# Keys of later chunks carried in the first low-rank step as well, and the activations transferred twice

## The chip, the cores and the metric

One NeuronCore of a Trainium2 chip runs the whole kernel. Its engines work side by side: TensorE (PE, with its weight loads shown apart as PEld), VectorE (DVE), ScalarE (ACT), GpSimd (POOL) and SyncE (SP), which issues nearly all DMAs. The metric is the device time of one execution in microseconds, as the median of several runs.

## The reference, cut to what matters

The block is a transformer layer on x of shape (2, 2048, 256), float32 throughout: a modulated layer norm, causal linear attention with 16 heads of width 16 and 128 random features, a residual, a second modulated norm, and a feed-forward layer of 1024 hidden channels with four low-rank experts of which two are taken.

```python
phi_q, phi_k = phi(q), phi(k)          # exp(x @ omega - |x|^2/2) / sqrt(128)
S = cumsum(phi_k[..., :, None] * v[..., None, :], axis=2)
Z = cumsum(phi_k, axis=2)
y = einsum('bhtm,bhtmd->bhtd', phi_q, S) / (einsum('bhtm,bhtm->bht', phi_q, Z)[..., None] + 1e-6)
x = x + ga * (y @ W_proj + b_proj)
h = layernorm(x) * (1 + cb) + sb
base, lora = h @ Wi.T, (h @ A) @ B     # lora for each of four experts
out = sum over the two best experts of  w_e * (relu(base + lora_e) @ Wo.T)
x = x + gb * out
```

## The kernel before, in words

The 4096 tokens are cut into N = 8 blocks of 512 tokens (four chunks of 128). Heads are taken in NG = 4 groups of four. A block has 16 (group, chunk) steps, done two chunks at a time: PAIRS = 8 pairs, one for each value of k in the main loop over i (block) and k (pair); the text calls one turn of that loop a slot. In slot (i, k) the attention of pair k of block i is finished, the scores of the following pair are prepared, and beside it run pieces of the neighbours: projections of block a = i + 1, norm, router and the first hidden unit of p = i - 1, the remaining hidden units of q = i - 2. Which piece stands where is written out by hand in run_full, and keep_written_order makes each engine run its instructions exactly as written. Every wait is therefore paid where it stands, with everything behind it on that engine.

A pair needs its keys turned, tokens by features. There are two ways. `turn` takes the exponentials phi and transposes them on TensorE (keys, L500), after which ScalarE copies them (keep_keys, L542). `key_rows` (L522) instead multiplies the raw key features once more by omega, with the operands the other way round, in the upper half of the four PSUM banks that a hidden unit uses, and ScalarE takes the exponential (keep_key_rows, L532). Key rows use 32 rows of the array for each head, as low_step (L821) uses 16, so the four heads run beside each other. In before only the second low-rank step of a unit carries them, for the pair that follows, in blocks 2 to 6 at k = 0, 1, 2 and 7 (these are the late slots).

From the turned keys, increments (L576) makes the change of the state into the upper half of the py bank, keep_increments (L588) copies it to SBUF (tile ds), states (L597) transposes it in the next slot and adds it to S (L607). outputs (L621, L627) makes the pair's result, keep_outputs (L635) copies it. Then features (L476) fills four mm banks for the next group and exponentials (L487) reads them.

A hidden unit is hidden (L836, 16 matmul instructions into four mm banks), first (low_step, then ReLU on ScalarE, L850) and second (low_step again, then max and scale on VectorE, L864, into one of four r buffers, and an addition on GpSimd, L865). Something is put between first and second so that TensorE has work while ScalarE reads the banks. PSUM tiles come from two rings: mm with four banks, side with two. A tile takes the ring's oldest bank, and its first writer waits until all readers of the bank's previous tile are done.

A block's x is loaded once, two blocks ahead (load, L99), into one of five xt buffers. It is used for the first norm (norm1), gets the projection's bias on GpSimd (add_bias, L370) at k = 6 of the block before, and is the residual in project (L682, L686) and finish (L874, L879) until store. At the end of the program, after the loop, come divide_invert of the last block (L660 to L666), three hidden units of block 6, divide (L675), project, norm2 and the rest of block 7.

Of the kernel before, what the change touches and what calls it, by code (L numbers as in the profile page):

```python
# [14 lines left out]
P = 128  # L15
# [17 lines left out]
def kernel(  # L33
# [58 lines left out]

    def load(i, pieces=1):
        b, blk = divmod(i, NBLK)
        xt = work.tile([P, NT, C], FP, tag="xt", name=f"xt{i}", bufs=5)
        src = x[b, blk * TB : (blk + 1) * TB, :].rearrange("(t p) c -> p t c", p=P)
        n = NT // pieces
        for t in range(0, NT, n):
            nc.sync.dma_start(xt[:, t : t + n, :], src[:, t : t + n, :])  # L99
        st[i] = {"x": xt}  # L100


    w_sb = const.tile([P, KC, 3 * C], FP, name="w_sb")
# [63 lines left out]

    def second_columns():

        second_row = work.tile([P, P], FP, tag="kt", name="second_row", bufs=1)  # L170
# [294 lines left out]
        )  # L465


    S, phi, turned, staged, y = {}, {}, {}, {}, {}

    def features(i, g, side):  # L470
        f = st[i]["feat"][side, g]
# [18 lines left out]
    def carried(i, t):  # L490

        return (i % NBLK, t) != (NBLK - 1, NT - 1)

    def keys(i, g, t, tile):

        if not carried(i, t):
            return
        pk = tile(f"pk{i}_{g}{t}")
        for j in range(HG):
            nc.tensor.transpose(  # L500
                pk[:, j * P : (j + 1) * P], phi[i, g, 1, j][:, t * P : (t + 1) * P], ident
            )
        turned[i, g, t] = pk
# [3 lines left out]
    def key_tile(i, g, t):  # L507

        n = (i, g, t // 2)
        if n not in pair:  # L510
            pair.clear()
            pair[n] = work.tile([P, 2, HG, M], FP, tag="kt", name=f"kt{i}_{g}{t}", bufs=1)
        return pair[n][:, t % 2]

    def key_rows(chunks, banks):


        for j, bank in enumerate(banks):
            rs = slice(2 * DH * j, 2 * DH * (j + 1))
            for i, g, t in chunks:  # L520
                c0 = TH + (t % 2) * P
                nc.tensor.matmul(  # L522
                    bank[:, c0 : c0 + P], st[i]["feat"][1, g][rs, t * P : (t + 1) * P], om[rs, :],
                    start=False, stop=True, skip_group_check=True, tile_position=(2 * DH * j, 0),
                )

    def keep_key_rows(chunks, banks):
# [36 lines left out]
        )  # L564
        staged[i, g, t] = am

    raised, before = {}, {}

    def increments(chunks, bank):

        cols = bank[:, TB // 2 : TB].rearrange("p (c m) -> p c m", m=P)
# [8 lines left out]
                )  # L580
        return ready, cols

    def keep_increments(ready, cols):
        if not ready:
            return
        i, g, t = ready[0]
        d = work.tile([P, 2, P], FP, tag="ds", name=f"ds{i}_{g}{t}")
        nc.vector.tensor_copy(d[:, 0 : len(ready), :], cols[:, 0 : len(ready), :])  # L588
        for n, chunk in enumerate(ready):
            raised[chunk] = d[:, n, :]  # L590
# [248 lines left out]
                )  # L839
        s["unit"][u] = (banks, f0, ts, whole_banks)  # L840

    def first(i, u):
        s = st[i]
        banks, f0, ts = s["unit"][u][0:3]
        low_step(s, 0, banks, f0, ts)
        for j, ph in enumerate(banks):
            f = f0 + j
            if f not in s["g"]:
                s["g"][f] = work.tile([P, TB], FP, tag="g", name=f"g{i}_{f}", bufs=NF)
            nc.scalar.activation(s["g"][f][:, ts], ph, AF.Relu)  # L850

    def second(i, u, chunks=()):

        s = st[i]
        banks, f0, ts, whole_banks = s["unit"].pop(u)
        if chunks:
            key_rows(chunks, whole_banks)
        low_step(s, 1, banks, f0, ts)
        if chunks:
            keep_key_rows(chunks, whole_banks)  # L860
        for j, ph in enumerate(banks):
            g = s["g"][f0 + j][:, ts]
            r = work.tile([P, TH], FP, tag="r", name=f"r{i}_{u}{j}", bufs=RG)
            nc.vector.scalar_tensor_tensor(r, ph, 0.0, s["rho"][:, ts], ALU.max, ALU.mult)  # L864
            nc.gpsimd.tensor_add(g, g, r)  # L865
# [77 lines left out]

    PAIRS = NG * NT // 2

    def run_full(i, k, turn, state, following):


# [20 lines left out]

        def unit_keys(of, which, *between):  # L970

            first(of, which)
# [97 lines left out]
    def behind(i, k):  # L1070
# [1 line left out]
        if 1 <= p < N and k == 5:  # L1072
            choose(p)
        if i + 2 < N:
            if k == 1 and i != 1:
                load(i + 2)
        if i == 0 and k == 6:
            load(3)
        if a < N and k == 6:
            if i == 0:  # L1080
                add_bias(0)
            add_bias(a)
        if i < N and k == PAIRS - 1:
            divide_load(i)

# [5 lines left out]
    for i in range(N):  # L1091
        for k in range(PAIRS):
# [146 lines left out]
```

## Time and profile before

| what | value |
|---|---|
| median of 3 runs | 758.28 us (758.04 to 760.54) |
| the profiled execution's own time | 756.79 us |
| its span, first to last instruction | 755.0 us |
| mean granted TensorE clock | 1.000 |
| instructions in the span | 24542 |
| key transposes L500 | 328, 137 ns of busy time each (44.9 us) |
| key rows L522 | 304, 47 ns each (14.4 us) |
| HBM | 35.32 MB read, 28.57 MB written |

A row of the timeline gives the start and the length in microseconds, the engine, the line of the kernel, the operation, the tiles written and read with their shapes, the number of instructions merged into the row, and in square brackets how long the engine stood idle before it and what released it. A row of the waits gives the engine and line that waited, what for, the total, the count and the longest. A matrix product in float32 is two instructions in the trace, a transpose one. Matmuls overlap in the array, so the length of one is not what it adds to a sequence: this text measures sequences from the start of one row to the start of another, most often on PEld.

### The profile page before, as it was taken

The numbers are of one execution on the slowest core, as the hardware profiler recorded it, in microseconds if no ns is written. First come the engines' busy times: TensorE is split into PE (matmuls) and PEld (weight loads), VectorE is DVE, ScalarE is ACT, GpSimd is POOL, SyncE is SP. The second block draws the span as 40 slices with busy tenths as digits, with TensorE's granted clock in tenths as the row PEclk, the third lists the DMA queues.
The fourth block names the chain that finished last, engine by engine and source line by source line (L and its number), as shares of the span: only waits on it lengthen the run. The fifth ranks groups of instructions, "written<-read, shape, count | busy, mean of one in ns | idle before, by whom it ended". The sixth has DMA issues, their size and how long they took to land.

```text
span 755.0 us, 24542 instructions
## 1 busy us (share of the span) xinstructions
PE 744.8 (99%) x10720; PEld 552.1 (73%) x10720; DVE 407.0 (54%) x1133; ACT 329.6 (44%) x742; POOL 148.3 (20%) x192
## 2 busy tenths in 40 slices
PE   9999999999999999999999999999999999999998
PEld 6667776666787767776787677877688777777776
DVE  5667667564663547534656456645364424654612
ACT  1665546535544444435544455435454343521010
POOL 3000322222210322011220122103130112005122
PEclk9999999999999999999999999999999999999999
DMA  4369443123301433023420342204240130002000
GB/s 134 111 195 298 146 143 100 44 82 120 114 29 32 129 112 114 17 72 119 124 72 33 111 125 82 67 29 130 73 127 16 50 110 17 16 34 83 1 29 28
DMA packets 44234, 65.46 MB, mean 87 GB/s; under 512 B 6752, under 2 KB 20256, under 8 KB 44128
## 3 DMA queue, kind: packets, MB, share of 16 engines
q1 hardware_dynamic: 42240, 62.33, 26.1%
q8 instruction: 84, 1.38, 0.8%
q10 hardware_dynamic: 1888, 1.58, 0.7%
q14 instruction: 22, 0.18, 0.1%
HBM read 35.32 MB, written 28.57 MB: 85 GB/s over the span
## 4 chain that ended last, share of the span: by engine, by line
PE 93%; DVE 4%; ACT 1%; issue 1%; DMA 0%; POOL 0%; DVEq 0%
PE ph L836 13%; PE pf L874 12%; PE pa L552 9%; PE pp L476 9%; PE pq L384 7%; PE ph L821 4%; PE pk L500 4%; PE pv L457 4%; PE py L621 4%; PE py L576 4%; PE py L627 3%; PE po L682 3%; PE pt L597 3%; PE pf L896 2%; PE ph L522 2%; PE pta L331 1%
## 5 line engine op out<-in xcount | busy, mean ns | idle before, releaser
L865 POOL TENSOR_TENSOR g<-g,r 128x256 f32<-128x256 f32 x128 | 90.6, 741 | 416.3 <-DVE r L864 416.3
L487 ACT ACTIVATE phi<-pp,lnm 128x512 f32<-128x512 f32 x256 | 155.2, 689 | 9.7 <-PE pp L476 3.6
L874 PE MATMUL pf<-wo_g,g 128*128 128x256 f32 x448 | 103.6, 382 | 0.4 <-ACT phi L487 0.2
L836 PE MATMUL ph<-h,wi_sb 128*128 128x256 f32 x448 | 101.9, 380 | 0.1
L836 PEld LDWEIGHTS ph<-h,wi_sb 128*128 128x128 f32 x448 | 84.3, 190 | 12.5 <-DVE r L864 0.5
L874 PEld LDWEIGHTS pf<-wo_g,g 128*128 128x128 f32 x448 | 82.6, 190 | 13.7 <-issue 2.2
L552 PEld LDWEIGHTS pa<-phi,phi 128*32 128x32 f32 x4096 | 77.5, 110 | 14.8 <-issue 13.3
L552 PE MATMUL pa<-phi,phi 128*32 128x128 f32 (+3 forms) x4096 | 85.4, 235 | 0.1
L850 ACT ACTIVATE g<-ph 128x256 f32<-128x256 f32 x112 | 33.9, 389 | 115.1 <-PE ph L821 115.1
L635 ACT COPY y<-py 128x128 f32<-128x128 f32 x128 | 27.8, 269 | 125.2 <-DVE ds L588 123.4
L561 DVE TENSOR_TENSOR am<-pa,causal 128x512 f32<-128x512 f32 x128 | 81.8, 681 | 0.0
L391 DVE TENSOR_SCALAR qs<-pq,bqk 128x512 f32<-128x512 f32 x30 | 22.5, 751 | 99.3 <-PE pq L384 94.6
L476 PE MATMUL pp<-f,om 32*128 32x512 f32 x512 | 73.6, 640 | 0.0
L542 ACT COPY kt<-pk 128x512 f32<-128x512 f32 x82 | 44.5, 594 | 54.8 <-PE pk L500 54.7
L864 DVE SCALAR_TENSOR_TENSOR r<-ph,rho 128x256 f32<-128x256 f32 x112 | 41.7, 422 | 45.6 <-PE ph L821 23.2
L384 PE MATMUL pq<-hT,w_sb 128*128 128x512 f32 x120 | 58.5, 612 | 0.0
L588 DVE COPY ds<-py 128x256 f32<-128x256 f32 (+1 forms) x63 | 25.7, 407 | 52.6 <-PE py L627 47.0
L621 PE MATMUL py<-am,v 128*32 128x128 f32 x1024 | 51.4, 273 | 0.0
L627 PE MATMUL py<-phi,S 128*32 128x128 f32 x960 | 50.1, 273 | 0.0
L597 PEld LDWEIGHTS pt<-ident,ds 128*128 128x128 f32 x120 | 12.8, 140 | 44.6 <-DVE ds L588 38.7
L500 PE MATMUL pk<-ident,phi 128*128 128x128 f32 x328 | 44.9, 275 | 0.5 <-ACT phi L487 0.4
L500 PEld LDWEIGHTS pk<-ident,phi 128*128 128x128 f32 x328 | 37.7, 141 | 7.1 <-ACT phi L487 3.0
(159 smaller groups left out, 968.2 us busy)
## 6 DMA issues: line engine op xcount, KB each, us to landing
f<-qd SPq DMA_DIRECT2D x60, 256.0 KB
qd<-qs SPq DMA_DIRECT2D x58, 256.0 KB
ydr<-y SPq DMA_DIRECT2D x32, 256.0 KB
num<-ydr SPq DMA_DIRECT2D x16, 256.0 KB
inv<-rdr SPq DMA_DIRECT2D x16, 256.0 KB
xt<-in_x_dram SPq DMA_DIRECT2D x7, 512.0 KB
out_dram<-xt SPq DMA_DIRECT2D x7, 512.0 KB
wo_g<-in_woT_dram SPq DMA_DIRECT2D x2, 1024.0 KB
```

The lines of the kernel that those rows point to most:

```text
L384: nc.tensor.matmul(pq, w_sb[:, k, n * P : (n + 1) * P], s["hT"][:, k, :], start=(k == 0), stop=(k == KC - 1),)
L476: nc.tensor.matmul(pp, om[rs, :], f[rs, :], start=True, stop=True, tile_position=(2 * DH * j, 0))
L487: nc.scalar.activation(ph, pps[j], AF.Exp, bias=lnm)
L500: nc.tensor.transpose(pk[:, j * P : (j + 1) * P], phi[i, g, 1, j][:, t * P : (t + 1) * P], ident)
L542: nc.scalar.copy(kt.rearrange("p h m -> p (h m)"), turned[i, g, t])
L552: nc.tensor.matmul(pa[t % 2][c * CG : (c + 1) * CG, j * P + q0 : j * P + q1], phi[i, g, 1, j][:, t0 + c * CG : t0 + (c + 1) * CG], phi[i, ...
L561: nc.vector.tensor_mul(am, pa[t % 2][:].rearrange("p (h q) -> p h q", h=HG), causal[t % 2][:].unsqueeze(1).to_broadcast([P, HG, P]),)
L621: nc.tensor.matmul(py[rows[j], :], v[:, t, g * HG + j, :], am[:, j, :], start=True, stop=state is None,)
L627: nc.tensor.matmul(py[rows[j], :], state[:, rows[j]], phi[i, g, 0, j][:, tok], start=False, stop=True,)
L836: nc.tensor.matmul(ph, wi_sb[:, k, f * P : (f + 1) * P], s["h2"][:, k, ts], start=(k == 0), stop=False, skip_group_check=True,)
L865: nc.gpsimd.tensor_add(g, g, r)
L874: nc.tensor.matmul(po, s["g"][f][:, t * P : (t + 1) * P], wo_g[i // NBLK][:, f, :], start=(f == 0), stop=(f == NF - 1), skip_group_check=True,
```

## The change: what it does

The first low-rank step of a unit now carries keys as well, for a pair some five pairs ahead (ahead): at k = 7 for pair 4 of the next block, at k = 0, 1 and 2 for pairs 5, 6 and 7 of the same block, in blocks 2 to 6. Their increments are made in the same slot into a second side bank (pe) and kept in a new tile dl (four buffers) until their pair comes; `keys` then skips them. The second step writes its key rows after the low-rank step, with start=True, since the banks' upper halves have been used in the meantime. In slots 0, 1, 2 and 7 the value matmuls (v) move from before the unit, or before the hidden layer, to between first and second.

kt gets two buffers and dl four. For that room, x from block 2 on is loaded into one xn buffer for the norm, and a second time as the residual (load_residual) into one of two xt buffers, at k = 0 of the next block (load_residual(p) with p = i - 1), with its bias added at k = 1; for the last block both stand after the loop, behind divide_invert.

```diff
+        if i < 2:
+            xt = work.tile([P, NT, C], FP, tag="xt", name=f"xt{i}")
+        else:
+            xt = work.tile([P, NT, C], FP, tag="xn", name=f"xn{i}", bufs=1)
...
+    def load_residual(i):
+        b, blk = divmod(i, NBLK)
+        xt = work.tile([P, NT, C], FP, tag="xt", name=f"xt{i}")
+        nc.sync.dma_start(
+            xt, x[b, blk * TB : (blk + 1) * TB, :].rearrange("(t p) c -> p t c", p=P)
+        )
+        st[i]["x"] = xt
...
-        if not carried(i, t):
+        if not carried(i, t) or (i, g, t) in raised:
             return
...
-    def first(i, u):
+    def first(i, u, chunks=()):
         s = st[i]
+        banks, f0, ts, whole_banks = s["unit"][u]
         low_step(s, 0, banks, f0, ts)
+        if chunks:
+            key_rows(chunks, whole_banks, False)
         for j, ph in enumerate(banks):
...
             nc.scalar.activation(s["g"][f][:, ts], ph, AF.Relu)
+        if chunks:
+            keep_key_rows(chunks, whole_banks)
 
     def second(i, u, chunks=()):
...
-        if chunks:
-            key_rows(chunks, whole_banks)
         low_step(s, 1, banks, f0, ts)
         if chunks:
+            key_rows(chunks, whole_banks, True)
             keep_key_rows(chunks, whole_banks)
...
+    def ahead(i, k):
+        if not (1 < i < N - 1 and k in (0, 1, 2, 7)):
+            return []
+        b, m = (i + 1, 4) if k == 7 else (i, 5 + k)
+        g, t = m // 2, 2 * (m % 2)
+        return [(b, g, u) for u in (t, t + 1) if carried(b, u)]
...
-                ((channels1, a), (hidden, q, 1), s, (v, 0), (unit_keys, q, 1, (qk, 2))),
-                (s, (v, 1), (hidden, q, 2), (unit_keys, q, 2, (qk, 0))),
-                (s, (v, 2), (hidden, q, 3), (unit_keys, q, 3, (qk, 3))),
+                ((channels1, a), (hidden, q, 1), s, (unit_keys, q, 1, (v, 0), (qk, 2))),
+                (s, (hidden, q, 2), (unit_keys, q, 2, (v, 1), (qk, 0))),
+                (s, (hidden, q, 3), (unit_keys, q, 3, (v, 2), (qk, 3))),
...
-                ((weigh, p, side_tile), (state, mm_tile), (ff, 3, mm_tile, 0, NF), (v, 3),
-                 (hidden, p, 0), (unit_keys, p, 0, (qk, 1))),
+                ((weigh, p, side_tile), (state, mm_tile), (ff, 3, mm_tile, 0, NF),
+                 (hidden, p, 0), (unit_keys, p, 0, (v, 3), (qk, 1))),
...
-            if k == 1 and i != 1:
+            if k == (i != 1):
                 load(i + 2)
         if i == 0 and k == 6:
-            load(3)
-        if a < N and k == 6:
-            if i == 0:
-                add_bias(0)
+            add_bias(0)
             add_bias(a)
+        if i > 2:
+            if k == 0:
+                load_residual(p)
+            elif k == 1:
+                add_bias(p)
...
+            early = ahead(i, k)
+            if early:
+                second_bank = side_tile(f"pe{i}_{g}{t}")
+                added_early = increments(early, second_bank)
             keep_increments(*added)
+            if early:
+                keep_increments(*added_early, "dl", 4)
...
     divide_invert(p)
+    load_residual(p)
+    add_bias(p)
     hidden(q, 1, other_set("last1"))
```

More of the change, by code (lines that the diff above doesn't have):

```diff
@@ L94, in load @@
         b, blk = divmod(i, NBLK)
-        xt = work.tile([P, NT, C], FP, tag="xt", name=f"xt{i}", bufs=5)
+        if i < 2:
+            xt = work.tile([P, NT, C], FP, tag="xt", name=f"xt{i}")
+        else:
+            xt = work.tile([P, NT, C], FP, tag="xn", name=f"xn{i}", bufs=1)
         src = x[b, blk * TB : (blk + 1) * TB, :].rearrange("(t p) c -> p t c", p=P)
@@ L168, in second_columns @@
     def second_columns():
-        second_row = work.tile([P, P], FP, tag="kt", name="second_row", bufs=1)
+        second_row = work.tile([P, P], FP, tag="kt", name="second_row")
         nc.vector.memset(halves(second_row[:])[:, :, 0, :], 0.0)
@@ L465, in values @@
         )
-    S, phi, turned, staged, y = {}, {}, {}, {}, {}
+    S, phi, turned, staged, y, raised, before = {}, {}, {}, {}, {}, {}, {}
     def features(i, g, side):
@@ L511, in key_tile, with key_rows @@
             pair.clear()
-            pair[n] = work.tile([P, 2, HG, M], FP, tag="kt", name=f"kt{i}_{g}{t}", bufs=1)
+            pair[n] = work.tile([P, 2, HG, M], FP, tag="kt", name=f"kt{i}_{g}{t}")
         return pair[n][:, t % 2]
-    def key_rows(chunks, banks):
+    def key_rows(chunks, banks, start):
         for j, bank in enumerate(banks):
@@ L523, in key_rows @@
                     bank[:, c0 : c0 + P], st[i]["feat"][1, g][rs, t * P : (t + 1) * P], om[rs, :],
-                    start=False, stop=True, skip_group_check=True, tile_position=(2 * DH * j, 0),
+                    start=start, stop=True, skip_group_check=True, tile_position=(2 * DH * j, 0),
                 )
@@ L565, in mask @@
         staged[i, g, t] = am
-    raised, before = {}, {}
     def increments(chunks, bank):
@@ L581, in increments, with keep_increments @@
         return ready, cols
-    def keep_increments(ready, cols):
+    def keep_increments(ready, cols, tag="ds", bufs=2):
         if not ready:
@@ L586, in keep_increments @@
         i, g, t = ready[0]
-        d = work.tile([P, 2, P], FP, tag="ds", name=f"ds{i}_{g}{t}")
+        d = work.tile([P, 2, P], FP, tag=tag, name=f"{tag}{i}_{g}{t}", bufs=bufs)
         nc.vector.tensor_copy(d[:, 0 : len(ready), :], cols[:, 0 : len(ready), :])
@@ L840, in hidden @@
         s["unit"][u] = (banks, f0, ts, whole_banks)
-    def first(i, u):
+    def first(i, u, chunks=()):
         s = st[i]
-        banks, f0, ts = s["unit"][u][0:3]
+        banks, f0, ts, whole_banks = s["unit"][u]
         low_step(s, 0, banks, f0, ts)
+        if chunks:
+            key_rows(chunks, whole_banks, False)
         for j, ph in enumerate(banks):
@@ L970, in unit_keys @@
         def unit_keys(of, which, *between):
-            first(of, which)
+            first(of, which, ahead(i, k))
             for do, *args in between:
```

## The prediction

> **What bounds the kernel now.** I read the engine totals of the page first, then its chain of waits, then the list of waits, then the timeline of one steady block (the one from 335 to 425 us), of the last block's end, and the busy windows there.
>
> ```profile
> PE 744.8 (99%) x10720; PEld 552.1 (73%) x10720; DVE 407.0 (54%) x1133; ACT 329.6 (44%) x742; POOL 148.3 (20%) x192
> ...
> PE 93%; DVE 4%; ACT 1%; issue 1%; DMA 0%; POOL 0%; DVEq 0%
> ```
>
> TensorE is busy 99% of the span and is 93% of the chain: an instruction taken from it is worth its time, one added costs it, and any new wait in its order is paid in full. The clock row shows 9 in all slices. So I count start to start on TensorE's load row, where the order is visible, and look for waits that the new order opens.
>
> ```profile
> 347.19 0.31 PEld L476 LDWEIGHTS pp<-f,om 32*128 32x128 f32 x8 [0.20 <-DVE r L864]
> 348.26 0.20 PEld L597 LDWEIGHTS pt<-ident,ds 128*128 128x128 f32 x2 [0.76 <-DVE ds L588]
> 348.43 0.73 PEld L457 LDWEIGHTS pv<-w_sb,hT 128*128 128x128 f32 x4
> 349.19 3.43 PEld L836 LDWEIGHTS ph<-h,wi_sb 128*128 128x128 f32 x16
> 352.94 0.31 PEld L821 LDWEIGHTS ph<-lT,lb_sb 16*128 16x128 f32 x8 [0.33 <-issue]
> ...
> 355.50 0.56 PEld L522 LDWEIGHTS ph<-om,f 32*128 32x128 f32 x16 [0.76 <-ACT g L850]
> 355.94 0.34 PEld L821 LDWEIGHTS ph<-lT,lb_sb 16*128 16x128 f32 x8
> 356.61 0.48 PEld L552 LDWEIGHTS pa<-phi,phi 128*32 128x32 f32 x26 [0.33 <-issue]
> ```
>
> This is pair 1 of a block. The reader sees the price of key rows: a low-rank step alone takes 353.59 - 352.94 = 0.65 us (the next row is the L384 load at 353.59), one with 16 key-row instructions takes 356.61 - 355.50 = 1.11 us. And the order at its start: features (L476), state transposes (L597), values (L457), hidden layer (L836).
>
> **Transposes removed.** Pairs 4 to 7 of five blocks lose their key transposes: 20 pairs, two of them with one chunk only, 38 chunks, 152 of the 328 transposes of L500. In the four slots concerned eight of them take 0.97 us from L500's first load or matmul to the next line's, less the switch (393.23 to 394.41 with 0.17 us idle). 152 / 8 x 0.97 = -18.4 us.
>
> **Key rows added.** 38 chunks x 8 instructions = 304, in the first low-rank step, at 1.11 - 0.65 = 0.46 us for 16: +8.7 us.
>
> **Increments moved.** Their number stays. Sixteen take 0.44 us at the end of the late slots (8 in 0.22) and 0.39 us where they went (378.16 to 378.53, 396.09 to 396.53): +1.0 us. The second copy of 0.42 us on VectorE lies behind features and is due a slot later: nothing; without that cover it would cost 20 x 0.42 = 8 us.
>
> **Values moved.** In pairs 1 and 2 the four value matmuls (0.76 us of loads) leave their place between state transposes and hidden layer. What is late next: the hidden layer writes the four banks that the features have just filled, so its first matmul needs the first exponential (L487) to have read its bank. The trace shows such a wait:
>
> ```profile
> 654.96 2.42 ACT L487 ACTIVATE phi<-pp,lnm 128x512 f32<-128x512 f32 x4 [0.26 <-PE pp L476]
> ...
> 655.69 0.42 PEld L500 LDWEIGHTS pk<-ident,phi 128*128 128x128 f32 x4 [0.30 <-ACT phi L487]
> ```
>
> The bank is released 0.73 us after the exponentials begin. In pair 1 above they begin at 348.35 (ACT row of the same timeline), so the hidden layer can start at 349.08, against 348.43 once the values are gone and 349.19 now. Only 0.11 us are won there, while the values cost 0.76 to 0.87 us in their new place: +0.68 us, ten times, +6.8 us. Lower end 0 (the wait falls under loads fetched ahead), upper end 8.7. I take 6.8: the release row is the same kind of bank. In pairs 0 and 7 other work stands before the hidden layer and the move is free.
>
> What the moved values are to cover: ScalarE must read the four new key banks before the second low-rank step may write them. Four ReLUs take 1.21 us and four key exponentials 1.55 us (350 us region, L850 and L532). Beginning 1.0 us after the first step they end at 3.8; TensorE comes back after 1.11 + 0.87 + 1.91 = 3.9 us. I take 0, upper end 20 x 0.3 = 6 us.
>
> **Router weights.** In slot 6 the transposes removed stood before low_rank:
>
> ```profile
> 402.74 0.46 DVE L782 COPY los<-los 128x216 f32<-128x216 f32 x2
> ...
> 403.20 0.91 PEld L793 LDWEIGHTS pl<-ident,los 128*128 128x128 f32 x8
> ```
>
> L793 follows VectorE's last copy at once. TensorE would now arrive 0.98 + 0.44 = 1.42 us earlier; VectorE, freed of the increments' copy (masks from 397.2 instead of 398.1), only 0.9 to 1.0 us earlier: 0.4 us x 5 = +2.0 us, between 0 and 6.
>
> Loop: -18.4 + 8.7 + 1.0 + 6.8 + 2.0 = +0.1 us.
>
> **Edits without a price.** ScalarE trades 38 copies (L542, 594 ns) for 80 exponentials (L532, 471 ns), both well inside the 2 to 4 us for which it idles in a slot; were that idle time gone, the early exponentials would cost 20 x 1.55 = 31 us, which is why the third rival below is theirs. The swapped order in the second step has the same 24 instructions. A second side bank per late pair needs L391's read of it, which ends 2 us before. kt and dl have a buffer for each tile alive.
>
> **Second transfer of x.** Six loads of 512 KB are added. In the loop the residual is issued on SP behind inv (SP's row at 351.8) and the bias add runs on POOL a slot later, behind the four L865 that end at 360.8; project reads x at 373. Ten us of cover: nothing. If it were gone, each would cost up to its landing time, 4 us x 5. The bias add (L370, 2.37 us) now meets VectorE's L675 at 360.86. The profile has L675 at 684 ns in the median and 1209 ns at most, so +0.5 us for each on VectorE, whose next result (S, 362.7) is needed at 365.6: nothing on the path.
>
> The Trainium skill, "SBUF — State Buffer", section "SBUF: two separate sides", is sharper: VectorE with two SBUF inputs and GpSimd hold one port pair exclusively, the loser blocked for the whole instruction. By it L675 could stand still for the full bias add, which still ends inside those 2.9 us; the sum stays.
>
> At the end nothing covers it. The last residual load is issued after divide_invert, and its bias add is queued on POOL ahead of all the L865 of block 6:
>
> ```profile
> 687.76 1.21 SPq L666 DMA_DIRECT2D inv<-rdr  x2
> ...
> 692.65 1.42 DVE L864 SCALAR_TENSOR_TENSOR r<-ph,rho 128x256 f32<-128x256 f32 x4 [3.51 <-PE ph L821]
> 693.98 2.33 DVE L675 TENSOR_TENSOR num<-num,inv 128x512 f32<-128x512 f32 x2
> ```
>
> SP gets to it at 689.0. The windows show inv's traffic until about 692.6 (DMA share 0.13 in 692 to 694, then 0.00); 512 KB at the 347 GB/s seen at 363 us are 1.5 us, and a reader is released some 1 us later (den, 32 KB, took 2.2 us from issue at 681.58 to its reader): landing at 695, an estimate, between 692.7 (2.2 + 1.5, nothing ahead) and 696.5. POOL then adds the bias (2.37) and only then runs the four L865 of unit 1 (2.79 in the trace, at 688.29), which hold the four r buffers. VectorE's L864 of unit 2 need these, and L675, the projection and the second norm wait behind them on VectorE. The last L864 ends at 695 + 2.37 + 2.79 + 0.5 = 700.7 instead of 694.07: +6.6 us (4.3 to 8.1). TensorE stands meanwhile, because the projection reads num; VectorE's chain of the norm then leads to the end, where TensorE already waits for it.
>
> By the Trainium skill's fit in "DMA: Bandwidth & Descriptors", section "Anatomy of one DMA", a transfer takes 2.0 us plus its bytes at 436 GB/s. An estimate from it alone is 3.2 us, landing at 692.2, a tail of +3.8 and a sum of +3.9 us; it leaves out the queue that the windows show.
>
> **Sum.** +0.1 + 6.6 = +6.7 us on a profiled execution of 756.79 us (span 755.0, 1.8 us around it): 763.5. The runs' median is 758.28, 1.5 us above it, so I predict 765.0 us. About 0.3% (2.3 us) is what a measurement of this kernel can tell from no change.
>
> **Rivals.**
> *Faster: the state's wait goes.* The waits list has L597 waiting for L588 38.7 us in 51 times, 0.76 each. With increments kept a block's half ahead, 20 such waits vanish; were they lost time, -15.2 + 6.7 gives 749.8. It decides if TensorE is idle in them. Against it: the matmul row has no such wait at all, the features' own matmuls (L476) run 1.14 us and fill it, and the same 0.76 stands where the releaser is "issue". Chance 0.10.
>
> *About the same: one of the two new waits is covered.* If the banks are free (-6.8) or the last load lands before POOL needs it (-6.6), 758.3. For the first speaks that loads may be fetched ahead; against the second, SP's own place at 689. Chance 0.17.
>
> *Slower still: ScalarE bounds the units.* If the second low-rank step waits for the early exponentials, +6 us: 771. The margin of 0.1 us speaks for it, the bank-by-bank order of the step against it. Chance 0.15.
>
> *That few keys are carried early* would leave 176 transposes unreached; the conditions fix 38 chunks, so I give it no share.
>
> The forecast has 0.58. Its own range takes the tail between its ends (-2.3, +1.5) and the router weights from 0 to 4 us (-2, +2): 760.7 to 768.5. Reaching to the second rival and the third gives 757 to 771. Faster by over 0.3% takes the first rival and a little of the second, 0.11; within 0.3% 0.16; slower 0.73.
>
> **What the profile would show.** Right: L500 x176, L522 x608; L836's load in pairs 1 and 2 waiting for L487, 0.6 to 0.7 us; L793 waiting for L782 about 0.4 us; in the last 80 us a bias add on POOL ending near 697 (in before's time), L864 idle for POOL some 6 us, and the stretch after the last pair 6 to 7 us longer while a steady block keeps its 89 us (inv is issued at 351.1, 440.2 and 529.7). Wrong: steady blocks shorter by over 1 us each, or L821 waiting for the new exponentials, or a bias add that POOL runs before L865 would have begun.

## The result and the profile after

The changed kernel takes 767.73 us in the median of six runs (765.56 to 771.22), the kernel before 758.16 us (six runs, 757.67 to 760.54). The ratio is 1.0128, with a 95% interval of 1.0109 to 1.0148: slower, by about 9.6 us. The forecast was 765.0 us with a range of 757 to 771; its own range, without the rivals, was 760.7 to 768.5. The profiled execution took 769.55 us, its span is 767.8 us. Lines are numbered anew; where the text needs it, the old number stands behind: scores L564 (552), features L488 (476), exponentials L499 (487), transposes L512 (500), key rows L534 (522) and their exponentials L544 (532), low-rank steps L831 (821), hidden layer L846 (836), ReLU L863 (850), max and scale L878 (864), GpSimd's addition L879 (865), bias add L382 (370), router weights L803 (793), increments L586 (576) and their copy L598 (588), state transposes L607 (597), the outputs' copy L645 (635), the division L685 (675), the projection L692 (682) and the second layer L888 (874).

The page of after: engine totals, the granted clock, HBM bytes and the chain of waits by engine.

```profile
PE 747.5 (97%) x10872; PEld 555.5 (72%) x10872; DVE 416.6 (54%) x1133; ACT 337.3 (44%) x784; POOL 148.3 (19%) x192
...
PEclk8999999999999999999999999999999999997999
...
HBM read 38.46 MB, written 28.57 MB: 87 GB/s over the span
...
PE 90%; DVE 3%; issue 3%; ACT 3%; DMA 1%; POOL 0%; SPq 0%; DVEq 0%; POOLq 0%
```

TensorE runs 152 instructions more: 304 key rows added (608 instead of 304), 152 transposes removed (176 instead of 328), both as forecast. HBM reads grew by 3.14 MB, the six loads of x. TensorE's share of the span falls from 99% to 97%, its share of the chain from 93% to 90%, and the clock row, which was 9 throughout, has an 8 in the first slice and a 7 in the slice from 691 to 710 us.

The same steady pair as before the change, pair 1 of a block (here block 5), on the load row of the timeline:

```profile
440.54 0.31 PEld L488 LDWEIGHTS pp<-f,om 32*128 32x128 f32 x8 [0.20 <-issue]
441.61 0.20 PEld L607 LDWEIGHTS pt<-ident,ds 128*128 128x128 f32 x2 [0.76 <-ACT y L645]
442.44 3.32 PEld L846 LDWEIGHTS ph<-h,wi_sb 128*128 128x128 f32 x16 [0.62 <-ACT phi L499]
446.09 0.31 PEld L831 LDWEIGHTS ph<-lT,lb_sb 16*128 16x128 f32 x8 [0.33 <-issue]
446.42 0.76 PEld L534 LDWEIGHTS ph<-om,f 32*128 32x128 f32 x16
447.30 0.73 PEld L469 LDWEIGHTS pv<-w_sb,hT 128*128 128x128 f32 x4
...
450.07 0.31 PEld L831 LDWEIGHTS ph<-lT,lb_sb 16*128 16x128 f32 x8 [0.76 <-ACT kt L544]
450.40 0.76 PEld L534 LDWEIGHTS ph<-om,f 32*128 32x128 f32 x16
451.28 1.20 PEld L564 LDWEIGHTS pa<-phi,phi 128*32 128x32 f32 x64
```

The values (L469) stand behind the key rows now, and the hidden layer waits 0.62 us for the first exponential, where before it had no wait. A low-rank step with keys takes 447.30 - 446.09 = 1.21 us and 451.28 - 450.07 = 1.21 us; with the key rows in front it took 1.11 us before.

The end of the program, from the timeline of after:

```profile
692.18 1.21 SPq L676 DMA_DIRECT2D inv<-rdr  x2
693.44 0.46 SPq L109 DMA_DIRECT2D xt<-in_x_dram  x1
...
699.24 2.34 POOL L382 TENSOR_TENSOR xt<-xt,bp_g 128x1024 f32<-128x1024 f32 x1 [14.12 <-DMA xt<-in_x_dram]
701.54 6.41 POOL L879 TENSOR_TENSOR g<-g,r 128x256 f32<-128x256 f32 x8
...
702.30 0.42 DVE L878 SCALAR_TENSOR_TENSOR r<-ph,rho 128x256 f32<-128x256 f32 x1 [9.10 <-POOL g L879]
...
702.78 3.06 PEld L888 LDWEIGHTS pf<-wo_g,g 128*128 128x128 f32 x8 [6.13 <-DVE r L878]
702.78 3.78 PE L888 MATMUL pf<-wo_g,g 128*128 128x256 f32 x8 [5.72 <-DVE r L878]
```

The chain can be read off from top to bottom: SP issues the second load of x when inv is out, GpSimd's bias add starts 5.8 us later, only then come GpSimd's additions for unit 1, only these free the r buffers for VectorE's unit 2, and TensorE stands until the first of these is done: its loads are idle for 6.13 us, its matmuls for 5.72 us.

Where the time went is read from the times between the scores (L564) of successive pairs, and from the last pair's scores to the end of the last matmul. "No early keys" below is the changed kernel without the early keys, an experiment that follows.

| stretch, us | before | after | no early keys |
|---|---|---|---|
| start to the first scores | 28.0 | 29.3 | 29.2 |
| a steady block (block 5, scores to scores) | 89.57 | 90.25 | 91.25 |
| all of blocks 2 to 7 | 511.3 | 514.2 | 519.1 |
| last scores to the end of the last matmul | 87.8 | 96.7 | 95.2 |

The same times for each pair of block 5, from its scores to those of the next pair. These stretches are called slots from here on; the products that a loop turn makes behind its scores fall into the next of them, so the early increments of k = 7, 0, 1 and 2 stand in stretches 0 to 3.

| stretch of block 5, us | 0 | 1 | 2 | 3 | 4 | 5 | 6 | 7 |
|---|---|---|---|---|---|---|---|---|
| before | 12.88 | 12.00 | 12.00 | 8.57 | 9.21 | 8.70 | 9.52 | 16.69 |
| no early keys | 12.97 | 12.75 | 12.75 | 8.57 | 9.22 | 8.70 | 9.52 | 16.78 |
| after | 14.03 | 13.75 | 13.75 | 8.13 | 7.91 | 7.39 | 8.39 | 16.90 |

Of the 2.9 us by which blocks 2 to 7 grew, 1.6 us lie in one slot of block 7 (13.26 to 14.90 us) in which the granted clock is halved for 3.4 us. The start has 6.8 us of half clock in after and none is recorded in before, but the traces without half clock there vary too, from 27.8 to 28.6 us, so not all of its 1.3 us need come from the clock. So the profiled execution lost 1.3 us in the loop, 8.9 us at the end and 2.9 us in these two places. These sum to 13.1 us against 12.8 us between the two spans; blocks 0 and 1 gave 0.2 us back.

### The profile page after: what moved, and what is told of

It reads as the page before. It is cut to its first block, busy times and chain, and to the rows that moved or that the text cites. A ratio compares the mean times of both kernels' runs of the same rounds, so it can differ in the third digit from the quotient of the medians.

```text
span 767.8 us, 24881 instructions
## 1 busy us (share of the span) xinstructions
PE 747.5 (97%) x10872; PEld 555.5 (72%) x10872; DVE 416.6 (54%) x1133; ACT 337.3 (44%) x784; POOL 148.3 (19%) x192
## 4 chain that ended last, share of the span: by engine, by line
PE 90%; DVE 3%; issue 3%; ACT 3%; DMA 1%; POOL 0%; SPq 0%; DVEq 0%; POOLq 0%
PE ph L846 13%; PE pf L888 12%; PE pa L564 9%; PE pp L488 9%; PE pq L396 7%; PE ph L831 5%; PE pv L469 4%; PE po L692 4%; PE py L631 4%; PE py L637 3%; PE ph L534 3%; PE py L586 2%; PE pk L512 2%; ACT phi L499 2%; PE pt L607 2%
## 5 line engine op out<-in xcount | busy, mean ns | idle before, releaser
L879 POOL TENSOR_TENSOR g<-g,r 128x256 f32<-128x256 f32 x128 | 90.6, 740 | 414.6 <-DVE r L878 414.6
L499 ACT ACTIVATE phi<-pp,lnm 128x512 f32<-128x512 f32 x256 | 155.1, 689 | 27.5 <-PE pp L488 25.6
L888 PE MATMUL pf<-wo_g,g 128*128 128x256 f32 x448 | 105.3, 387 | 6.4 <-DVE r L878 5.7
L846 PE MATMUL ph<-h,wi_sb 128*128 128x256 f32 x448 | 103.2, 383 | 4.1 <-ACT phi L499 4.0
L888 PEld LDWEIGHTS pf<-wo_g,g 128*128 128x128 f32 x448 | 83.7, 193 | 20.4 <-DVE r L878 6.1
L846 PEld LDWEIGHTS ph<-h,wi_sb 128*128 128x128 f32 x448 | 83.5, 190 | 18.5 <-ACT phi L499 6.8
L645 ACT COPY y<-py 128x128 f32<-128x128 f32 x128 | 27.8, 269 | 137.0 <-DVE ds L598 84.8
L564 PEld LDWEIGHTS pa<-phi,phi 128*32 128x32 f32 x4096 | 78.1, 110 | 11.4 <-issue 7.4
L564 PE MATMUL pa<-phi,phi 128*32 128x128 f32 (+3 forms) x4096 | 86.1, 236 | 0.1
L863 ACT ACTIVATE g<-ph 128x256 f32<-128x256 f32 x112 | 33.9, 389 | 112.6 <-PE ph L534 81.9
L488 PE MATMUL pp<-f,om 32*128 32x512 f32 x512 | 73.2, 640 | 0.0
L878 DVE SCALAR_TENSOR_TENSOR r<-ph,rho 128x256 f32<-128x256 f32 x112 | 41.9, 422 | 51.4 <-ACT kt L544 22.0
L544 ACT ACTIVATE kt<-ph,lnm 128x256 f32<-128x256 f32 (+1 forms) x160 | 61.2, 480 | 0.0
L473 DVE TENSOR_TENSOR v<-pv,bv_bc 128x256 f32<-128x256 f32 x32 | 13.6, 424 | 82.4 <-PE pv L469 81.7
L396 PE MATMUL pq<-hT,w_sb 128*128 128x512 f32 x120 | 56.5, 594 | 0.0
L831 PE MATMUL ph<-lT,lb_sb 16*128 16x256 f32 x448 | 41.2, 424 | 0.5 <-ACT g L863 0.5
L893 DVE TENSOR_TENSOR xt<-pf,xt 128x256 f32<-128x256 f32 x28 | 11.8, 423 | 51.8 <-PE pf L888 51.8
L617 DVE TENSOR_TENSOR S<-pt,S 128x128 f32<-128x128 f32 x112 | 31.8, 284 | 11.6 <-PE pt L607 9.7
```

The source lines that it names most:

```text
L396: nc.tensor.matmul(pq, w_sb[:, k, n * P : (n + 1) * P], s["hT"][:, k, :], start=(k == 0), stop=(k == KC - 1),)
L488: nc.tensor.matmul(pp, om[rs, :], f[rs, :], start=True, stop=True, tile_position=(2 * DH * j, 0))
L499: nc.scalar.activation(ph, pps[j], AF.Exp, bias=lnm)
L544: nc.scalar.activation(pair[i, g, t // 2][:, 0:n, j, :], bank[:, TH : TH + n * P].rearrange("p (n m) -> p n m", m=M), AF.Exp, bias=lnm,)
L564: nc.tensor.matmul(pa[t % 2][c * CG : (c + 1) * CG, j * P + q0 : j * P + q1], phi[i, g, 1, j][:, t0 + c * CG : t0 + (c + 1) * CG], phi[i, ...
L831: nc.tensor.matmul(ph, lb_sb[rs, (f0 + j) * P : (f0 + j + 1) * P], s["lT"][n][rs, ts], start=False, stop=True, skip_group_check=True, tile ...
```

## The experiments

My theory was the forecast's: early keys pay for what they cost, the wait of the hidden layer eats the remaining gain in the loop, and the whole loss is the second transfer of the last block's x at the end. After the traces one thing was added to it: that TensorE, idle for some 6 us at the end, then runs at half clock for a while. The rivals are named with each run.

**The last block keeps its x.** One block is normed last, so its first copy is still there; the sixth second transfer goes.

```diff
     divide_invert(p)
-    load_residual(p)
-    add_bias(p)
...
             add_bias(a)
+        if i == N - 2 and k == 6:
+            add_bias(a)
```

> The changed kernel, but the last block keeps the x that was loaded for its norm (its buffer is loaded by nobody afterwards): no sixth second transfer, and its bias is added in block 6 at k = 6 as in before. Theory (the last load holds up POOL, then VectorE, then TensorE): the stretch from the last scores to the end falls from 96.7 us back to before's 87.8, POOL's bias add at 699 is gone and with it L878's wait of 9.1 us, and the time is 767.7 - 8.9 = about 758.8 us. Rival (the five transfers inside the loop cost the time, by DMA traffic or by POOL's bias add beside VectorE's L685): only a sixth of 9.6 us goes, 766 us.

Measured: 759.12 us (ten runs, 758.07 to 760.54), 1.0012 times before (1.0001 to 1.0023). The stretch after the last scores is 87.8 us, that of before. Against after, 8.6 us are gone with one transfer and the place of one addition on GpSimd; over the 758.00 us of before, measured beside it, 1.1 us are left, and the loop has 1.3. The rival, that the five transfers in the loop cost the time, falls.

**The wait filled.** Twenty products of the identity with itself, 40 instructions into a bank half that nobody reads any more, stand where TensorE idles. The wait for GpSimd stays, and TensorE's idle time goes.

```diff
     first(q, 3)
+    for _ in range(20):
+        nc.tensor.matmul(pa[1][:, TH : TH + P], ident, ident, start=False, stop=True, ...)
     divide(p)
```

> The changed kernel with 20 idle products of the identity, 40 matmul instructions of about 0.114 us, put where TensorE waits at the end (after the first low-rank step of the third unit there), into an unused half of a bank. The wait for POOL stays. Theory (TensorE stood still for 5.7 us and was then granted half its clock for about 10 us, which makes the loss there 8.9 instead of 6.6 us): the granted clock in that stretch stays at 1.00 and the time falls by about 2.3 us, to 765.4. Rival (the loss beyond 6.6 us is VectorE's and GpSimd's, which run beside each other there): no change, 767.7, or a little more by the idle products.

Measured: 767.31 us (four runs, 763.83 to 769.37), 1.0111 (1.0075 to 1.0146). The median doesn't tell the two theories apart; it lies at the rival's. The profiled execution, at 763.83 us, is what carries a reading. This is the load row of its timeline:

```profile
694.83 4.54 PEld L1188 LDWEIGHTS pa<-ident 128*128 128x128 f32 x40 [1.13 <-ACT g L863]
699.29 1.60 PEld L888 LDWEIGHTS pf<-wo_g,g 128*128 128x128 f32 x8
...
702.07 0.30 PEld L692 LDWEIGHTS po<-wp_g,num 128*128 128x128 f32 x2 [0.53 <-DVE num L685]
```

The same eight loads of L888 take 1.60 us here and 3.06 us in after, the stretch after the last scores is 93.9 instead of 96.7 us, and the granted clock is 1.000 throughout. Between these two executions, 93.9 - 87.8 = 6.1 us is then the wait itself, and 2.8 us are half clock. Over all traces of this study the picture is the same: the four with the idle wait at the end (after, no early keys, values back, second transfer alone) have half clock in it, the six without the idle time (before among them) have none there. That is association in ten traces. The runs' mean clocks say the same: of the 18 runs of those four kernels none was granted 1.000 (0.987 to 0.998), of the 80 listed runs of the others 37 were. The three other runs of the filled kernel had mean clocks of 0.993, 0.998 and 0.996 and left no trace, so where they lost it, and whether filling helps in the median, is open.

**The second transfer alone,** applied to the kernel before, with its buffers and both its places.

```diff
+        if i < 2: xt = work.tile(..., tag="xt", ...)
+        else:     xt = work.tile(..., tag="xn", ..., bufs=1)
...
+            if k == 0: load_residual(p)
+            elif k == 1: add_bias(p)
...
     divide_invert(p)
+    load_residual(p)
+    add_bias(p)
```

> Before with the second transfer of x alone (one xn buffer, two xt buffers, residual loads and bias adds where the change has them); no early keys, values and increments as in before. Theory: slots as in before to 0.05 us, and the stretch from the last scores to the end 6.1 us longer by the wait and up to 2.8 us longer by the halved clock: 764 to 767 us. Rival (the second transfer disturbs the loop too): slots 0 and 1 of blocks 3 to 7 longer by 0.1 us or more.

Measured: 767.66 us (four runs, 765.01 to 769.29), 1.0107 (1.0077 to 1.0136). It alone gives the whole loss; the median lies 0.7 us above the range expected. The eight slots of block 5 take 12.88, 12.00, 12.00, 8.57, 9.21, 8.70, 9.52 and 16.69 us, each within 0.01 us of before. Blocks 2 to 7 take 513.0 us, of which 1.6 us lie in one slot of block 7 with half clock, as in after; without them it is 511.4 us against 511.3 before. So the five transfers in the loop cost nothing. The stretch after the last scores takes 97.9 us, 1.2 us more than in after, and TensorE's matmuls idle for 7.90 us in it. GpSimd's row at the end says why, with the same instruction as in after:

```profile
699.97 2.34 POOL L382 TENSOR_TENSOR xt<-xt,bp_g 128x1024 f32<-128x1024 f32 x1 [16.28 <-DMA xt<-in_x_dram]
```

**No early keys,** all else as changed.

```diff
     def ahead(i, k):
-        if not (1 < i < N - 1 and k in (0, 1, 2, 7)):
-            return []
+        return []
```

> The changed kernel without early keys: no pair is carried in the first step, pairs 4 to 7 are transposed as before, their increments are made where they were; the values stay where the change put them and x is still transferred twice. Theory (the keys save 18.4 us of transposes and cost 8.7 us of rows, 1 us of increments and some 2 us of waiting for the router weights): the changed kernel's time + about 7 us, 774 to 775. Rival (the carried keys save nothing on TensorE because the transposes lay beside waits): within 2 us of 767.7.

Measured: 775.50 us (four runs, 772.85 to 778.06), 1.0223 (1.0183 to 1.0264). The early keys are worth 7.8 us between the medians, and 519.1 - (514.2 - 1.6) = 6.5 us in the loop. The rival, that the carried keys save nothing on TensorE, falls. The load row of its pair 1 shows the hidden layer's wait unchanged, so the wait belongs to the moved values and not to the early keys:

```profile
443.61 3.32 PEld L846 LDWEIGHTS ph<-h,wi_sb 128*128 128x128 f32 x16 [0.63 <-ACT phi L499]
```

**The values back in their old place** in pairs 1 and 2.

```diff
-    (s, (hidden, q, 2), (unit_keys, q, 2, (v, 1), (qk, 0))),
+    (s, (v, 1), (hidden, q, 2), (unit_keys, q, 2, (qk, 0))),
-    (s, (hidden, q, 3), (unit_keys, q, 3, (v, 2), (qk, 3))),
+    (s, (v, 2), (hidden, q, 3), (unit_keys, q, 3, (qk, 3))),
```

> The changed kernel with the value matmuls of pairs 1 and 2 put back between state transposes and hidden layer, where before has them. Theory: the hidden layer's wait for the features' exponentials (0.62 us, ten times) goes, but the second low-rank step now comes 0.75 us earlier, while the fourth early key exponential ends only about 0.1 us before it in the changed kernel; it waits about as long instead. Slot by slot within 0.2 us, 766 to 768.5 us. Rival (the moved values were a plain loss of 0.68 us in ten slots, as the forecast summed it): 767.7 - 6.8 = 761 us.

Measured: 766.92 us (four runs, 764.88 to 769.66), 1.0111 (1.0074 to 1.0148), 0.8 us under after, which the intervals don't tell from nothing; the rival's 761 us falls. Slot 1 takes 13.73 us where after has 13.75. The load row of its pair 1:

```profile
441.31 3.43 PEld L846 LDWEIGHTS ph<-h,wi_sb 128*128 128x128 f32 x16
...
448.19 0.95 PEld L831 LDWEIGHTS ph<-lT,lb_sb 16*128 16x128 f32 x7 [0.76 <-ACT kt L544]
450.03 1.20 PEld L564 LDWEIGHTS pa<-phi,phi 128*32 128x32 f32 x64
```

The hidden layer no longer waits, but seven loads of the second low-rank step take 0.95 us where eight took 0.31, and the step with its key rows takes 450.03 - 448.19 = 1.84 us instead of 1.21. It now stands for the early exponentials, which have 0.75 us less beside them. The loss has changed its place, and in block 5 its size stays within 0.02 us a slot. Neither place of the values pays, so something else has to stand before the hidden layer.

**Early increments after the features** of pairs 0 and 1, in the kernel whose last block keeps its x. These sixteen products read kt and v and write the side bank, so they can stand between the features and the hidden layer.

```diff
             keep_increments(*added)
-            if early:
-                keep_increments(*added_early, "dl", 4)
+            if early and k not in (0, 1):
+                ... increments and keep_increments as before
...
             exponentials(*features(...))
+            if early and k in (0, 1):
+                second_bank = side_tile(...)
+                keep_increments(*increments(early, second_bank), "dl", 4)
```

> The kernel that keeps the last block's x (759.1 us), with the early increments of pairs 0 and 1 made after the features instead of ahead of them. Theory (in pairs 1 and 2 the hidden layer waits for the first exponential, which starts 1.2 us after the features whatever lies behind them): the features come 0.44 us earlier, the 16 increment instructions fill what was a wait of 0.62 us, and ten slots are 0.44 us shorter each: 759.1 - 4.4 = 754.7 us, with L846's wait for L499 at about 0.2 us. Rival (the wait is for ScalarE being late, by its copies L645 before the exponentials, and not for the features): no change, 759 us.

Measured: 755.35 us (twelve runs, 753.50 to 757.86), 0.9959 (0.9943 to 0.9975). Slots 1 and 2 of block 5 fall from 13.75 to 13.31 us, by 0.44 each, which is the whole length of the moved instructions: they vanish in the wait. Ten such slots would make 4.4 us; blocks 2 to 7 are 4.1 us shorter in the trace, one slot of block 7 with half clock apart. Between the medians of the two kernels lie 3.8 us, and 4.5 us when each is taken against the before measured beside it (758.00 and 758.71). In nine of the ten slots L846 has no wait for L499 left, in one 0.22 us. The rival, that the wait is for ScalarE being late and not for the features, would have changed nothing, and falls.

**Key rows ahead of the low-rank instructions** in the first step, in the kernel whose last block keeps its x.

```diff
     def first(i, u, chunks=()):
+        if chunks:
+            key_rows(chunks, whole_banks, False)
         low_step(s, 0, banks, f0, ts)
-        if chunks:
-            key_rows(chunks, whole_banks, False)
```

> The kernel that keeps the last block's x, with the key rows ahead of the low-rank instructions in the first step (their banks' upper halves are fresh there, so no start is needed). Theory (the order low-rank, then key rows takes 1.21 us in the trace of the changed kernel, the other order 1.11 us in that of before): 0.1 us less in each of 20 slots, 759.1 - 2.0 = 757.1 us. Rival (the 0.1 us belongs to what follows, values or scores, and not to the order): no change, 759 us.

Measured: 757.03 us (twelve runs, 755.51 to 760.56), 0.9971 (0.9953 to 0.9990). Late slots of block 5 fall by 0.10 us (14.03 to 13.93, 13.75 to 13.65). Over blocks 2 to 7 the trace is 1.7 us shorter, because two slots of block 3 don't fall. The median lies 2.1 us under the 759.12 us of the kernel it was made from, and 2.8 us when each is taken against the before measured beside it. The rival, that the 0.1 us belongs to what follows, falls. Its load row:

```profile
446.22 0.56 PEld L534 LDWEIGHTS ph<-om,f 32*128 32x128 f32 x16 [0.33 <-issue]
446.67 0.34 PEld L831 LDWEIGHTS ph<-lT,lb_sb 16*128 16x128 f32 x8
447.33 0.73 PEld L469 LDWEIGHTS pv<-w_sb,hT 128*128 128x128 f32 x4 [0.33 <-issue]
```

447.33 - 446.22 = 1.11 us for the same 24 instructions that take 1.21 us the other way round.

**All three edits together.**

> The two edits together: last block's x kept, early increments of pairs 0 and 1 after the features, key rows ahead of the low-rank instructions in the first step. Theory: 759.1 - 4.4 - 2.0 = 752.7 us, 0.7% under before. Rival: the second low-rank step then waits for the early key exponentials, which end about 0.1 us ahead of it now, and the 2.0 us are lost again: 754.7 us.

Measured: 752.83 us (six runs, 751.66 to 755.30), 0.9919 (0.9895 to 0.9942): faster than both kernels, by 5.9 us than the before measured beside it (758.71 us). The steady block takes 89.00 us (90.25 in after, 89.57 before), with slots 1 and 2 at 13.22 us: both gains stay, and the rival's 754.7 us falls. The load row of its pair 1, where the increments L586 stand before the state transposes and the hidden layer has no wait left:

```profile
437.24 0.31 PEld L488 LDWEIGHTS pp<-f,om 32*128 32x128 f32 x8 [0.20 <-issue]
438.31 0.38 PEld L586 LDWEIGHTS pe<-kt,v 128*32 128x32 f32 x16 [0.76 <-issue]
438.88 0.20 PEld L607 LDWEIGHTS pt<-ident,ds 128*128 128x128 f32 x2 [0.20 <-issue]
439.13 3.32 PEld L846 LDWEIGHTS ph<-h,wi_sb 128*128 128x128 f32 x16
```

## Why the prediction was right, and where it was off

**The end, +6.6 us: right in its chain and its size.** By the start of the denominators' arithmetic on VectorE (L660 at 683.78 before, L670 at 687.82 after), after runs 4.0 us late when the end begins. Forecast was that the load lands at 695 in before's time, 699.0 in after's; GpSimd's bias add, which waits for it, starts at 699.24. The last max and scale of the four then ends at 704.77, which is 700.7 in before's time, the very figure of the forecast, and the filled kernel puts the wait at 6.1 us. One reason in the chain was wrong: the forecast had TensorE stand because the projection reads num. It stands one product earlier, at L888 for VectorE's L878, as the rows of the end show, and L888 is done when the projection starts at 707.66. By the Trainium skill's fit ("DMA: Bandwidth & Descriptors", section "Anatomy of one DMA — SWDGE (gpsimd) path") an estimate of the load's time is 3.2 us. That section gives the fit for transfers issued by GpSimd, and this one is issued by SyncE. It took 5.8 us from its issue to its reader, and the windows from 694 to 698 us move 0.95 MB, about inv's 512 KB and its own, so the measurement decides for the queue.

**Half clock: missing.** The sum lacks a term of about 2.2 us: 9.6 between the medians, less 6.1 at the end and 1.3 in the loop. The wait was priced at its length, as if TensorE came back from it as it went in. The busy windows of after show otherwise (columns: window, length, busy time and instructions of PE, PEld, DVE, ACT and POOL, granted clock, DMA share, GB/s):

```profile
698.00:700.00 2.00, 0.00 (x0) 0.00 (x0) 0.00 (x0) 0.28 (x2) 0.76 (x1) 1.00 0.05 18
700.00:702.00 2.00, 0.00 (x0) 0.00 (x0) 0.00 (x0) 0.00 (x0) 2.00 (x2) 0.79 0.00 0
702.00:704.00 2.00, 1.22 (x3) 1.04 (x4) 1.19 (x3) 0.00 (x0) 2.00 (x4) 0.50 0.00 0
...
710.00:712.00 2.00, 2.00 (x8) 1.65 (x7) 1.29 (x5) 0.00 (x0) 1.51 (x3) 0.65 0.00 0
```

TensorE idles from 697.1 to 702.8. The window from 700 to 702 lacks 0.21 of the full clock and the one from 710 to 712 lacks 0.35, so the clock is halved from about 701.2 to 711.4, beginning 4.1 us into the idle time. The second-layer products and most of the projection run in that stretch. The Trainium skill has the rule ("TensorE: Matmul & The Clock Gate", section "What's actually happening"): the clock is gated to half after an idle window of about 3.4 us, in windows that run freely, and comes back after a busy one. The trace of after agrees, with 3.41 us without any matmul ahead of the half clock and 10.24 us of it, three times 3.41 us. The second transfer alone agrees less well: TensorE idles there from 695.6 to 703.5, and this window already has the clock halved from about 698.1, only 2.5 us into the idle time:

```profile
698.00:700.00 2.00, 0.00 (x0) 0.00 (x0) 0.00 (x0) 0.00 (x0) 0.03 (x1) 0.53 0.05 17
```

There the measurement decides. Had the forecast laid that rule on its own 6.6 us of idle time, it would have looked for this. That the 2.2 us between the medians are half clock is not shown: what is shown is 2.8 us between two profiled executions, and the filled kernel's median stayed where it was.

**The loop, +1.3 us against +0.1: close, with several terms mis-sized.** The transposes and key rows came in the numbers forecast. The slots that lose eight transposes and 16 increments (4, 5 and 6) fall by 1.31, 1.31 and 1.13 us from no early keys to after, against 0.97 + 0.44 = 1.41 in the forecast. Slot 3 loses eight transposes, gains 16 increments and falls by 0.44. Eight transposes were thus worth some 0.87 us; the lines that the forecast names for them give 1.01, not its 0.97. What the early keys bring in all is 6.5 us, against 18.4 - 8.7 - 1.0 - 2.0 = 6.7. That these agree is partly luck. In block 5 the early keys bring 91.25 - 90.25 = 1.0 us, where the forecast's terms give 4 x (0.97 - 0.46 - 0.05) - 0.4 = 1.4; block 3, and blocks 2 and 7 together, bring 1.7 and 1.5, which is not explained here. By the table the key rows cost 0.56 us a slot instead of 0.46, and the increments next to nothing instead of 0.05 (0.44 more in slots 0 to 3, 0.44 less in 4 to 7). The term that failed most clearly is in the edits without a price: "The swapped order in the second step has the same 24 instructions." It has, and they take 1.21 us instead of 1.11. In the first step the same 0.10 us is in the price of the key rows, which was read from the old order. The order costs up to 0.1 us in 2 x 20 steps, 4 us; the run with the rows first took back most of the half that it touched, and the second step was not tried.

**Values moved, +6.8 us: right in wait, place and nearly in size.** Here are four of the waits of after (who waits for whom, then the total in us, the count and the longest), the last of them on the matmul row:

```profile
PEld ph L846 <- ACT phi L499: 6.8, 12, 0.7
PEld ph L831 <- ACT kt L544: 15.2, 20, 0.8
PEld pl L803 <- issue: 2.0, 6, 0.4
PE ph L846 <- ACT phi L499: 4.0, 10, 0.5
```

That the hidden layer's waits sum to 6.8 us is chance. Two of the twelve stand in other slots, as before the change, and on the matmul row the ten are 4.0 us. What shows the size is slot 1 without early keys, 12.75 - 12.00 = 0.75 us longer than before, of which 0.09 is the order, as slot 0 shows: 0.66 for a forecast of 0.68. Over all ten slots it is 6.2 us.

**The router weights, +2.0 us: too dear, the cause not shown.** The third line has 2.0 us, five waits of 0.36 us in the loop and one at the end, and it names "issue" where I had named VectorE's copy. The matmul row has no idle time there. What slot 6 shows is a fall 0.18 us smaller than that of slots 4 and 5, some 0.9 us in five blocks.

**The third rival, ScalarE,** looks fulfilled in the second line: 20 waits of 0.76 us for the key exponentials. It isn't. The second step had the same 0.76 us before the change, behind the ReLU (355.50 in the lines of the prediction), and no early keys shows it with "issue". The matmul row of after has no idle time at these twenty places, so by that row nothing was lost there. The exponentials end at 449.93 and the step begins at 450.07, so the margin was indeed 0.1 us, and the run with the values back shows what happens when it is gone.

**The first rival, the state's wait,** is answered the same way. The waits of L607 for ds fell from 38.7 us in 51 to 15.2 us in 20, and no slot shortened by more than its transposes and increments: in the lines of pair 1 above the same 0.76 us stands, with ScalarE's y as its releaser. Under all names together the load row stood before the state's transposes for 44.1 us in 58 waits in before, and for 44.0 us in 58 in after. The second rival, that one of the two new waits is covered, falls by the rows above: L846 waits in every one of its ten slots, and the last load lands too late for GpSimd.

**The transfers in the loop** were forecast to cost nothing, and the second transfer alone shows it within 0.01 us a slot of block 5. One detail under it was mis-sized. The bias add was to cost VectorE 0.5 us for each L685 that it meets; in the timeline of block 5 of after, GpSimd and VectorE together, it is more:

```profile
455.35 2.36 POOL L382 TENSOR_TENSOR xt<-xt,bp_g 128x1024 f32<-128x1024 f32 x1
...
455.97 2.89 DVE L685 TENSOR_TENSOR num<-num,inv 128x512 f32<-128x512 f32 x2
```

Two L685 take 2.89 us, against 2 x 0.68 at their median; the first takes 2.29 us and ends 0.55 us after the bias add does. Five L685 of the trace, each beside a bias add, take 2.15 to 2.29 us, where before the longest was 1.21. That is nearer to the Trainium skill's rule weighed in the prediction ("SBUF — State Buffer", section "SBUF: two separate sides"), the loser blocked for the whole instruction. VectorE idles for 2.83 us soon after, before its next work at 462.22, and the slots show nothing of it.

## What to carry to other kernels

A step that is free in every turn of a loop can be dear once behind it: one transfer out of six cost 6.1 us and all that follows, and keeping one buffer gave it back. Price a wait of TensorE with what stands behind it, and if it is as long as the 5.5 to 7.9 us of the four kernels here, also with the clock afterwards. Before a gap like the 0.62 us of the hidden layer is accepted, look for work that is already there and free of the banks concerned; here sixteen increments, 0.44 us of the order, fitted into it without a remainder.

## What was unexpected of the hardware

Half clock comes in pieces of 3.41 us: 6.8, 3.4 and 10.24 us in the profiled execution of after. Those at the start and in one slot of block 7 come in some executions and not in others, and they are part of why single runs of one kernel lie up to 7 us apart; what sets them off was not found. A long idle time is not what all of them follow: in the five traces that have the one in block 7, TensorE was busy for 2.90 of the 3.41 us ahead of it, while in the run with the rows first 2.09 us of idle time at 107.75 were followed by none. At the end, half clock began 2.5 to 4.1 us into the idle time; it came back after one stretch of 3.41 us with TensorE busy throughout in three traces, and in after only after two.

Two groups of instructions that use 32 and 16 rows of the array take 1.11 us when the 32-row group goes first, and 1.21 us when it goes second, and the row shows the difference in the 32-row group's loads: 0.56 us for sixteen when first, 0.76 us when second. Why is open.

The list of waits names the last releaser of an idle load row. Here an idle time of 0.76 us on the load row stood under several names (the ReLU, the key exponential, the state's copy, ScalarE's y, and issue), and taking a name away took no time away; the matmul row had no idle time there.
